# Reordering the first routing of a two-layer MoE kernel, with planner costs for a change of matmul shape

## The chip, the cores and the metric

The kernel runs on one core of one Trainium2 chip. The metric is the device time of one execution in microseconds. The kernel before takes 512.19 us (median of three runs, 511.12 to 512.78).

## The reference

The input `x` is 8 sequences of 256 rows of 128 numbers, 2,048 rows in all. Two layers follow; only the first is touched here. In shortened form:

```python
def moe(x):                                  # one weight set, used twice
    normed = rmsnorm(x) * norm_weight
    probs  = softmax(normed @ router.T)      # 8 experts
    w, idx = top_k(probs, 2); w /= w.sum()
    return x + alpha * sum_over_chosen(w_e * down_e(silu(gate_e(normed)) * up_e(normed)))

x = x + 0.5 * moe(layernorm(x))              # MoE layer r0
x = x + attention(layernorm(x))              # 16 heads of 8, causal
x = x + 0.5 * moe(layernorm(x))              # MoE layer r1
x = x + 0.5 * ffn(x); x = x + gated_shifts(x); x = x + 0.5 * ffn(x)   # the mixing stage
```

Each row goes to two of eight experts, so there are 4,096 pairs of a row and an expert, with a hidden size of 352.

## The kernel before, in words

**Groups and tiles.** The 2,048 rows are cut into four groups of 512 rows (`x[0]` to `x[3]`, each four tiles of 128 rows). An expert tile is 2 x 64 rows: the upper half belongs to one expert, the lower half to another. A MoE layer has 36 such tiles. The rows of each tile are gathered from memory by an index list (`take`), so the tiles can only begin when the list is known.

**Two plans in each MoE layer.** `moe_route(g, r)` normalises a group (`norm`), transposes it (`pt`), scales it (`nT`), computes the eight logits (`pl`) and takes the two topmost experts (`topmost`, the tiles `lg`, `top`, `which`). `moe_plan(r, False)` then builds the index list `take0` for the first 12 tiles from groups 0 and 1 alone; `moe_plan(r, True)` builds `take1` for the other 24 from all four groups. A plan is a chain of small steps on VectorE: marks (`wf`, `oh`, `m`), counts on TensorE (`pc`), a copy on ScalarE (`sums`), prefix sums on TensorE (`pp`), slots (`end` to `less`), `hit`, a product on GpSimd (`val`), comparisons `at` of 4 x 128 columns each (one set of the first plan on ScalarE, `ata`), and the sum `pi` on TensorE that turns them into `take`. Expert numbers come by a side path (`le`, `ef`, `pe`, `expert`).

**An expert tile.** `moe_experts` gathers (`xs`, an indirect DMA that GpSimd issues), transposes (`pt`), scales (`nT`). `moe_tile` copies the weights of the lower expert (`wg` 704 columns, `wd` 384 columns), multiplies (`pg`, `pu`, each as 64-row halves), applies Silu on ScalarE (`sg`), multiplies on VectorE (`hid`), transposes back on TensorE (`ph`), copies (`hT`) and multiplies down (`po`). `pg`, `pu` and `po` use 64 columns of the matmul array at a time; transposes and all other matmuls use another shape. A tile's `pg` is made to follow the `ph` of the tile two before it (line 1060).

**The order of the work.** Nothing waits in the program for what the planner writes: class `Work` (lines 117 to 253) is a list scheduler on the host. Each operation has an engine, an assumed cost and `needs`; its rank is the longest assumed path from it to the end, plus a bias (`w.back = -BIAS[..]`). `issue` picks the earliest start, or an operation of higher rank on the same engine that could start within 0.3 us of it. What comes out is the order of the instructions on each in-order engine. A need that is no real dependence therefore only moves an instruction in its queue. Where TensorE would stand idle, `keep_warm` issues dummy matmuls (`pw`). `either` lets the planner choose ScalarE or VectorE by the two costs given.

**Biases.** `BIAS[0..3]` lift the four groups in the last part of r1 and in the mixing stage, `BIAS[4]` the routing and first plan of r1, `BIAS[5]` its later groups and its whole plan, `BIAS[6]` the later groups and the whole plan of r0.

Of the kernel before, what the change touches and what calls it, by code (L numbers as in the profile page):

```python
# [19 lines left out]
P = 128  # L20
NG = 4
GT = 4
S = 256
E = 8
HID = 352
# [9 lines left out]

BIAS = (27.0, 38.0, 18.0, 10.0, 25.0, 29.0, 1.0)
HC = (0, 128, 224)
ROUND = float(3 * 2**22)  # L40
NH = 16
# [6 lines left out]
LN_EPS = 1e-5  # L48
RMS_EPS = 1e-6
# [58 lines left out]
class Op:  # L108
    def __init__(self, engine, us, do, needs, takes, uses, lag, spare):
        self.engine, self.us, self.do, self.lag, self.spare = engine, us, do, lag, spare  # L110
        self.takes, self.uses = takes, uses
        self.needs = [n for n in needs if n is not None]
        self.out, self.end, self.rank, self.back = None, None, None, 0.0
        self.choice = None


class Work:
# [9 lines left out]
    def __init__(self, buffers, free):  # L127
        self.ops, self.free, self.back = [], dict(free), 0.0
        self.buffers = {tag: [0.0] * n for tag, n in buffers.items()}
        self.idle = None  # L130

    def op(self, engine, us, do=None, needs=(), takes=(), uses=(), lag=0.0, spare=0):

# [22 lines left out]
    def start(self, op):  # L156
# [11 lines left out]
        op.engine, op.us = best[2], op.choice[best[2]]  # L168
        return best[1]

    def start_on(self, op):
        t = self.free.get(op.engine, 0.0)
        for n in op.needs:
            if isinstance(n, Op):
                t = max(t, n.end + self.gap(n, op))
        for buf in op.takes:
            slots = self.buffers[buf.tag]
            n = sum(b.tag == buf.tag for b in op.takes)
            if len(slots) < n + op.spare:
                return None  # L180
            t = max(t, sorted(slots)[n - 1])
        return t
# [5 lines left out]
    def keep_warm(self, a, b):  # L188
        slots = self.buffers["b"]
        us = self.WARM * (2 if a < self.COLD else 1)  # L190
        n = int((b - a - self.SLACK) / us)
        if n < 2 or min(slots) > a:
            return
        slots.remove(min(slots))
        slots.append(a + n * us)
        if self.idle is not None:
            self.idle(n)

    def issue(self):
        before = {}  # L200
        for op in self.ops:
            op.wait, op.rank = 0, 0.0
            before[op] = {n if isinstance(n, Op) else n.owner for n in op.needs} - {op}
            op.next = []
        for op in self.ops:
            op.wait = len(before[op])
            for n in before[op]:
                n.next.append(op)

        order, stack = [], [op for op in self.ops if op.wait == 0]  # L210
        left = {op: op.wait for op in self.ops}
        while stack:
            op = stack.pop()
            order.append(op)
            for n in op.next:
                left[n] -= 1
                if left[n] == 0:
                    stack.append(n)
        assert len(order) == len(self.ops), "operations need each other"
        for op in reversed(order):  # L220
            op.rank = op.us + max((n.rank + self.gap(op, n) for n in op.next), default=op.lag)
        for op in self.ops:
            op.rank -= op.back
        ready = [op for op in self.ops if op.wait == 0]
        while ready:
            starts = [(self.start(op), op) for op in ready]
            starts = [(t, op) for t, op in starts if t is not None]
            assert starts, "no buffer comes free"
            t, op = min(starts, key=lambda s: (s[0], -s[1].rank))
            for t2, op2 in starts:  # L230
                if op2.engine == op.engine and op2.rank > op.rank and t2 <= t + 0.3:
                    t, op = t2, op2
            ready.remove(op)
            if op.engine == "pe":
                self.keep_warm(self.free["pe"], t)
            for buf in op.takes:
                slots = self.buffers[buf.tag]
                slots.remove(min(slots))
            op.end = t + op.us
            if op.engine is not None:  # L240
                self.free[op.engine] = op.end
            if op.do is not None:
                op.out = op.do()
            for buf in (*op.uses, *(b for b in op.takes if b.left == 0)):
                buf.left -= 1
                buf.end = max(buf.end, op.end)
                if buf.left <= 0:
                    self.buffers[buf.tag].append(buf.end)
            for n in op.next:
                n.wait -= 1  # L250
                if n.wait == 0:
                    ready.append(n)
        return max(op.end for op in self.ops)
# [3 lines left out]
def tile_macaron(ctx: ExitStack, tc: tile.TileContext, a: dict, out: bass.AP):  # L257
# [22 lines left out]
    gu = ctile("gu", [P, E, 2 * HID])  # L280
    dw = ctile("dw", [P, E, len(HC), P])
# [18 lines left out]
    wd, wup, wuv, wo, wr, wkk, wv, vw, gw = (rest[:, c] for c in parts.values())  # L300
# [104 lines left out]
    def wtile(tag, name, shape, dtype=F32):  # L405
        return wk.tile(list(shape), dtype, tag=tag, name=name, bufs=len_of[tag])
# [17 lines left out]
    weights = w.op(None, 0.0, lag=24.0)  # L424
# [83 lines left out]
    def moe_layer(n, first):  # L508

        few = (4 * GT * first - 7) // 2  # L510

        soon = first + 1 if n == 1 and first + 1 < NG else None
        r = {
            "n": n, "first": first, "few": few, "soon": soon, "stored": {}, "all_stored": {}, "topped": {},
            "plan": {}, "hold": {},
        }
        for name, shape, dtype in (
            ("top", [P, NT, 8], F32), ("which", [P, NT, 8], U32), ("w", [P, NT, 2], F32),
            ("ab", [P, 2, NT], F32), ("rs", [P, NT], F32), ("slot", [P, 2 * NT], U32),
            ("take0", [P, few], U32), ("take1", [P, TILES - few], U32), ("expert", [1, 2 * TILES], I32),  # L520


            ("end", [P, E], F32), ("full", [P, 3, E], F32), ("base", [P, E], F32),
            ("both", [P, E], F32),
        ):
            r[name] = ctile(f"{name}_{n}", shape, dtype)
        for name, rows in (
            ("rows0", GT * first * P), ("rows1", NT * P), ("ys", TILES * P),
        ):
            r[name] = dram.tile([rows, P], F32, name=f"{name}_{n}", tag=f"{name}_{n}")  # L530
        return r

    def moe_route(g, r):


        n = 8 * r["n"] + g


        late = r["n"] == 0 and g >= 2
        y, filled = norm(  # L540
            g, n, "ep" if late else "y",
            (lambda: stile("ep", "ep", (P, 4, GT, P))[:, 0]) if late
            else lambda: wtile("y", "n", (P, GT, P)),
            eps=LN_EPS * RMS_EPS, scale=1.0 + RMS_EPS,
        )

        first = g < r["first"]
        to, rows = ("stored", "rows0") if first else ("all_stored", "rows1")
        aside = first and r["n"] == 0
        r[to][g] = (w.act if aside else w.sp)(  # L550
# [13 lines left out]
        b1, b2, nTb = Buf("b"), Buf("b"), Buf(tag)  # L564
# [26 lines left out]
                i = GT * g + t  # L591
                nc.vector.max_index(r["which"][:, i, :], r["top"][:, i, :], lg[:, t, :])

        r["topped"][g] = w.dve(1.3, topmost, pl, uses=[b2])

    def moe_weights(groups, r, behind):

# [58 lines left out]
    def moe_plan(r, whole):  # L656
# [248 lines left out]
        for k in range(2 * nt // GT):  # L905
            ab = Buf("ata" if k in by_act else "at")
            at = (w.act if k in by_act else w.dve)(
                1.6 if k in by_act else 0.68, lambda k=k: is_at(k), rowed, takes=[ab]
            )
            found = w.pe(  # L910
                0.3, lambda k=k, at=at: find(k, at), at, valued, found,
                **(dict(takes=[bi], uses=[ab]) if k == 0 else dict(uses=[ab, bi])),
            )
# [104 lines left out]
    def moe_tile(r, plan, k, nT, nb, j, pus, turned, downs, numbers):  # L1018
# [9 lines left out]
        def copied(engine, tag, src, width):  # L1028
            e = {"act": nc.scalar, "dve": nc.vector}[engine].number(
                r["expert"][0:1, 2 * k + 1 : 2 * k + 2]  # L1030
            )
            dst = wtile(tag, tag, (P, width))
            src = src[:, bass.ds(e, 1)].rearrange("p o h -> p (o h)")
            copies(engine, dst, src)
            return dst

        gb, db = Buf("wg"), Buf("wd")
        gates = w.either(
            1.15, 1.05, lambda e: copied(e, "wg", gu, 2 * HID), plan["experts"], weights,
            *pus[-3:-2], takes=[gb],  # L1040
        )
        backs = w.either(
            0.85, 0.76, lambda e: copied(e, "wd", dw.rearrange("p e c d -> p e (c d)"), len(HC) * P),
            plan["experts"], weights, *pus[-3:-2], takes=[db],
        )

# [14 lines left out]
                  takes=[bg], uses=[nb], spare=3)  # L1061
        pu = w.pe(0.6, lambda: product(1), pg, takes=[bu], uses=[nb, gb])
        pus.append(pu)

        def gate():
            sg = wtile("sg", "sg", (P, HID))
# [50 lines left out]

        po = w.pe(0.67, down, hT, backs, takes=[bo], uses=[tb, db])
        downs.append(po)

        def result(engine):
            ys = wtile("ys", "ys", (P, P))
# [755 lines left out]
```

## Time and profile before

| what | value |
|---|---|
| median of three runs | 512.19 us |
| the profiled execution | 510.68 us, of which span 508.5 us |
| TensorE busy | 485.4 us (95%), dummy matmuls included |
| VectorE, ScalarE, GpSimd busy | 351.0, 293.4, 224.9 us |
| first index list (`take`) written | at 24.91 us |
| first expert matmul (`pg`) | at 32.10 us |
| TensorE's work stops for r1's whole plan | 318.2 to 329.2 us, but for `pi` and `pe` |
| granted TensorE clock, mean | 0.98 |

The stages on this time axis: loading, routing and first plan of r0 up to 32 us; its expert tiles up to about 125 us; attention up to 300 us, with r1's first tiles among it from 285 us; r1's other tiles up to about 415 us; the mixing stage, overlapping, from about 406 us to the end. A row of the timeline reads: start in us, length in us, engine, line, operation, tile written<-tiles read, sizes, number of instructions merged into the row, and in brackets the idle time before it and what ended it.

### The profile page before, as it was taken

The page shows a single profiled execution, that of the slowest core. Times are in us where ns is not written, and L with a number is a line of the kernel's source. Part 1 is how long each engine was busy: PE and PEld are TensorE (multiplying, and loading weights), DVE is VectorE, ACT ScalarE, POOL GpSimd, SP SyncE. Part 2 cuts the span into 40 slices and gives each one's busy share as a digit, 9 for nine tenths or more (in the row PEclk, how much of TensorE's full clock was granted, in tenths as well). Part 3 has the DMA queues.
Part 4 walks back from the last instruction along what each step waited for, and adds up shares of the span by engine and source line. Part 5 has one row for each costly group of instructions (what it writes and reads, how often), then busy time and mean ns, then how long its engine had stood idle before and what let it go on. Part 6 is the DMA issues. An engine that isn't in the chain of part 4 may idle for free.

```text
span 508.5 us, 13883 instructions
## 1 busy us (share of the span) xinstructions
PE 485.4 (95%) x5206; PEld 312.9 (62%) x5206; DVE 351.0 (69%) x1217; ACT 293.4 (58%) x580; POOL 224.9 (44%) x240
## 2 busy tenths in 40 slices
PE   7978999999999999999999999599999998999995
PEld 4535666565666775776767766365666665566673
DVE  8788566476757986668786366935677755979770
ACT  3346676676355455455557566166767556586542
POOL 7084872563006600000027000278766568786731
PEclk9899999999999999999999999689999999999998
DMA  8941212231001100000201101022222111000001
GB/s 269 305 130 49 68 49 57 58 68 44 12 23 38 51 1 3 3 22 4 64 13 51 26 1 43 16 75 67 42 76 53 48 48 42 1 1 1 23 21 41
DMA packets 25984, 25.53 MB, mean 50 GB/s; under 512 B 3872, under 2 KB 23328, under 8 KB 25504
## 3 DMA queue, kind: packets, MB, share of 16 engines
q1 hardware_dynamic: 20368, 15.21, 9.7%
q0 software_dynamic: 4352, 8.92, 7.4%
q8 instruction: 42, 0.69, 0.6%
q10 hardware_dynamic: 1200, 0.53, 0.4%
q14 instruction: 22, 0.18, 0.1%
HBM read 16.78 MB, written 8.91 MB: 51 GB/s over the span
## 4 chain that ended last, share of the span: by engine, by line
PE 74%; DVE 11%; POOL 4%; issue 3%; ACT 1%; DMA 0%; POOLq 0%; ACTq 0%; DVEq 0%
PE sc L70 18%; PE po L70 15%; PE pg L70 9%; PE pu L70 9%; PE ph L70 6%; PE pt L70 5%; PE pgt L70 2%; DVE at L70 2%; PE pv L70 2%; POOL q L70 2%; PE pr L70 2%; PE pj L70 2%; POOL back L70 2%; DVE x L70 1%; PE pk L70 1%
## 5 line engine op out<-in xcount | busy, mean ns | idle before, releaser
L70 POOL DMA_INDIRECT xs<-rows,take x72 | 70.2, 976 | 48.3 <-issue 15.7
L70 POOL DMA_INDIRECT back<-ys,slot x64 | 61.3, 957 | 60.3 <-issue 45.4
L70 ACT ACTIVATE ep<-sc 128x512 f32<-128x512 f32 x96 | 52.3, 595 | 50.4 <-PE sc L70 46.8
L70 POOL TENSOR_TENSOR stats<-stats,minus_half 128x4 f32<-128x4 f32 x28 | 29.0, 1034 | 103.3 <-DVE stats L70 102.5
L70 DVE TENSOR_TENSOR hid<-sg,pu 128x352 f32<-128x352 f32 x71 | 36.8, 518 | 37.5 <-PE pu L70 35.9
L70 PEld LDWEIGHTS po<-dw,hT 128*64 128x64 f32 x432 | 49.9, 138 | 19.7 <-issue 15.9
L70 PE MATMUL po<-dw,hT 128*64 x432 | 60.0, 277 | 0.9 <-ACT sg L70 0.3
L70 PE MATMUL po<-wd,hT 128*64 128x128 f32 x432 | 60.1, 277 | 0.0
L70 ACT COPY wg<-gu 128x704 f32 x61 | 47.4, 779 | 19.7 <-PE pu L70 9.8
L70 PE MATMUL pg<-gu,nT 128*64 x144 | 57.4, 480 | 0.6 <-ACT nT L70 0.5
L70 PEld LDWEIGHTS sc<-kT,qT 32*128 32x128 f32 x768 | 46.0, 186 | 19.3 <-issue 17.3
L70 PE MATMUL pg<-wg,nT 128*64 128x352 f32 x144 | 57.4, 480 | 0.0
L70 PE MATMUL sc<-qT,kT 32*128 32x128 f32 x768 | 56.7, 283 | 0.0
L70 PE MATMUL pu<-wg,nT 128*64 128x352 f32 x144 | 56.2, 472 | 0.0
L70 PE MATMUL pu<-gu,nT 128*64 x144 | 56.2, 472 | 0.0
L70 PE MATMUL sc<-kT,qT 32*128 32x128 f32 x768 | 55.2, 284 | 0.0
L70 DVE TENSOR_REDUCE mtmp<-sc 128x4 f32<-128x512 f32 x64 | 41.4, 684 | 14.2 <-PE sc L70 14.0
L70 PEld LDWEIGHTS po<-wd,hT 128*64 128x64 f32 x432 | 49.9, 138 | 0.0
L70 PEld LDWEIGHTS sc<-qT,kT 32*128 32x128 f32 x768 | 47.4, 186 | 3.3 <-issue 2.1
L70 ACT ACTIVATE sg<-pg 128x352 f32<-128x352 f32 x72 | 33.4, 463 | 27.6 <-PE pg L70 22.3
L70 ACT COPY hT<-ph 128x384 f32<-128x384 f32 x56 | 26.7, 479 | 29.1 <-PE ph L70 27.5
L70 PE MATMUL ph<-ident,hid 128*128 128x128 f32 x216 | 39.2, 293 | 1.5 <-DVE hid L70 1.1
(227 smaller groups left out, 1056.1 us busy)
## 6 DMA issues: line engine op xcount, KB each, us to landing
ys<-ys SPq DMA_DIRECT2D x72, 64.0 KB, 1.5
gu<-in_guT SPq DMA_DIRECT2D x2, 1408.0 KB
rest<-in_rest SPq DMA_DIRECT2D x1, 1280.0 KB
xs<-rows,take POOLq DMA_INDIRECT x72
x<-in_x SPq DMA_DIRECT2D x4, 256.0 KB
dw<-in_dwT SPq DMA_DIRECT2D x1, 1024.0 KB
rows<-rows SPq DMA_DIRECT2D x2, 512.0 KB
back<-ys,slot POOLq DMA_INDIRECT x64
```

Of the source, the lines that this page charges most:

```text
L70: ins = do(*args, **kw)
```

## The change

Six edits, all in what the planner is told:

1. In `moe_route`, the moments of groups 2 and 3 of r0 are given a need on the normalised rows of groups 0 and 1 (`filled`).
2. The topmost experts of groups 2 and 3 of r0 are given a need on all comparisons `at`/`ata` of the first plan (`compared`).
3. `split=0` makes ScalarE normalise all four tiles of a group, where VectorE did two of them: groups 2 and 3 of r0, and groups 0 to 2 of r1.
4. The planner charges 0.1 us when TensorE changes between 64-column work (`strips`) and other work, and lets other work count as 0.1 us later still when it compares starts.
5. The assumed costs of the weight copies fall: `wg` from 1.15 and 1.05 us (ScalarE, VectorE) to 1.1 and 0.9, `wd` from 0.85 and 0.76 to 0.84 and 0.74.
6. The seven biases change.

```diff
-BIAS = (27.0, 38.0, 18.0, 10.0, 25.0, 29.0, 1.0)
+BIAS = (22.0, 28.0, 18.0, 12.0, 25.0, 34.0, -3.0)
...
+    SWITCH, STICK = 0.1, 0.1
+
     def start_on(self, op):
         t = self.free.get(op.engine, 0.0)
+        if op.engine == "pe" and op.us > 0.05 and op.strips != self.strips:
+            t += self.SWITCH
...
             starts = [(t, op) for t, op in starts if t is not None]
             assert starts, "no buffer comes free"
-            t, op = min(starts, key=lambda s: (s[0], -s[1].rank))
-            for t2, op2 in starts:
-                if op2.engine == op.engine and op2.rank > op.rank and t2 <= t + 0.3:
-                    t, op = t2, op2
+
+            starts = [
+                (t + self.STICK if op.engine == "pe" and op.strips != self.strips else t, t, op)
+                for t, op in starts
+            ]
+            at, t, op = min(starts, key=lambda s: (s[0], -s[2].rank))
+            for at2, t2, op2 in starts:
+                if op2.engine == op.engine and op2.rank > op.rank and at2 <= at + 0.3:
+                    at, t, op = at2, t2, op2
...
-            else lambda: wtile("y", "n", (P, GT, P)),
-            eps=LN_EPS * RMS_EPS, scale=1.0 + RMS_EPS,
+            else lambda: wtile("y", "n", (P, GT, P)), *r["filled"] if g >= r["first"] else (),
+            eps=LN_EPS * RMS_EPS, scale=1.0 + RMS_EPS, split=0 if late or r["n"] and g < NG - 1 else 2,
         )
 
         first = g < r["first"]
+        if first and r["n"] == 0:
+            r["filled"] += filled
...
-        r["topped"][g] = w.dve(1.3, topmost, pl, uses=[b2])
+        r["topped"][g] = w.dve(1.3, topmost, pl, *r["compared"], uses=[b2])
...
+            if r["n"] == 0 and not whole:
+                r["compared"].append(at)
...
         gates = w.either(
-            1.15, 1.05, lambda e: copied(e, "wg", gu, 2 * HID), plan["experts"], weights,
+            1.1, 0.9, lambda e: copied(e, "wg", gu, 2 * HID), plan["experts"], weights,
...
         backs = w.either(
-            0.85, 0.76, lambda e: copied(e, "wd", dw.rearrange("p e c d -> p e (c d)"), len(HC) * P),
+            0.84, 0.74, lambda e: copied(e, "wd", dw.rearrange("p e c d -> p e (c d)"), len(HC) * P),
...
         pus.append(pu)
+        pg.strips = pu.strips = True
...
         downs.append(po)
+        po.strips = True
```

The lines left out set `strips` to False at first, after dummy matmuls, and to that of the last TensorE operation issued.

More of the change, by code (lines that the diff above doesn't have):

```diff
@@ L113, in __init__ @@
         self.out, self.end, self.rank, self.back = None, None, None, 0.0
+        self.strips = False
         self.choice = None
@@ L129, in __init__ @@
         self.buffers = {tag: [0.0] * n for tag, n in buffers.items()}
-        self.idle = None
+        self.idle, self.strips = None, False
     def op(self, engine, us, do=None, needs=(), takes=(), uses=(), lag=0.0, spare=0):
@@ L195, in keep_warm @@
         slots.append(a + n * us)
+        self.strips = False
         if self.idle is not None:
@@ L235, in issue @@
                 self.keep_warm(self.free["pe"], t)
+                if op.us > 0.05:
+                    self.strips = op.strips
             for buf in op.takes:
@@ L514, in moe_layer @@
             "n": n, "first": first, "few": few, "soon": soon, "stored": {}, "all_stored": {}, "topped": {},
-            "plan": {}, "hold": {},
+            "plan": {}, "hold": {}, "filled": [], "compared": [],
         }
```

## Prediction

> **What bounds the kernel now.** I read the page's first two parts, then the chain that ended last, then the timeline of every stretch in which TensorE had no work of its own.
>
> ```profile
> PE 485.4 (95%) x5206; PEld 312.9 (62%) x5206; DVE 351.0 (69%) x1217; ACT 293.4 (58%) x580; POOL 224.9 (44%) x240
> PE   7978999999999999999999999599999998999995
> DVE  8788566476757986668786366935677755979770
> PEclk9899999999999999999999999689999999999998
> ```
>
> TensorE (PE) is the bound nearly everywhere: nines from 38 us on. The exceptions are the first three slices, one 5 at 318 to 330 us, and the end. But the first digits flatter it: until 32.1 us nearly all of its busy time is dummy matmuls (`pw`), so the first 32 us are a chain of small steps and no work of the experts. What that chain gains is carried to the end wherever TensorE has no slack: from 60 to 130 us it is busy 70.00 of 70 us, and from 130 to 190 us 59.78 of 60. So I ask first when the first expert matmul starts.
>
> ```profile
> 19.25 1.02 DVE L70 TENSOR_SCALAR at<-iota_r,row 128x128 f16<-128x128 f16 x4
> 20.20 0.18 DVE L70 COPY lg<-pl 128x32 f32<-128x32 f32 x1
> 21.24 0.17 DVE L70 COPY lg<-pl 128x32 f32<-128x32 f32 x1
> 22.28 1.37 DVE L70 TENSOR_SCALAR at<-iota_r,row 128x128 f16<-128x128 f16 x8
> 24.43 0.35 PE L70 MATMUL pi<-val,at 128*128 128x12 f16 x8
> 24.91 0.17 DVE L70 TENSOR_SCALAR take<-pi 128x12 uint32<-128x12 f32 x1 [0.93 <-PE pi L70]
> 25.39 1.32 POOL L70 DMA_INDIRECT xs<-rows,take  x1 [5.32 <-DVE wf L70]
> 31.34 0.30 PE L70 MATMUL pt<-ident,xs 128*128 128x128 f32 x1 [1.89 <-DMA xs<-rows,take]
> 32.10 0.51 PE L70 MATMUL pg<-gu,nT 128*64 x1 [0.46 <-ACT nT L70]
> ```
>
> Between the first comparison set and the other two, VectorE does the topmost experts of groups 2 and 3 (each begins with a `lg` copy): 20.20 to 22.28, 2.08 us that the first plan does not need. Then `pi` comes 0.78 us after the last `at` (23.65), since TensorE was inside 11 dummy matmuls until 24.4; they took 4.0 us, not the 2.2 us planned, because the granted clock was 0.50 between 22 and 24 us. `take` follows, the first gather, its landing, the first product.
>
> **Edit 2, topmost behind the comparisons.** With 2.08 us out of the way the two `at` sets run from 20.3 to about 21.7; ScalarE's set (`ata`) ends at 21.04 in this trace, so it is not late. The gap that called for the dummy matmuls shrinks from over 2 us to under 1, which gives back most of the 0.78: I take 0.6. `take` moves from 24.91 to 22.2, by 2.7 us (bounds 2.0 to 3.0). The moved instructions issue no DMA. Queued behind them on VectorE is the whole plan's first step (`wf`, at 25.00 now); 22.4 plus 2.08 is 24.5, so it is not later than before.
>
> **Edits 1 and 3 in r0.** Group 1's normalising on VectorE stood behind group 2's moments (7.01 to 8.27) though its own `pow` ended at 7.64. Moved, they give group 1 about 0.6 us, but its transposes then meet group 0's logits on TensorE (9.25 to 10.31), so 0.3 (0 to 0.6). The later `pow` steps stay hidden: GpSimd was idle from 11.8 to 19.4. On ScalarE, four tiles take 1.76 us in a block where two took 0.88. In this trace such a block (14.76 to 15.64) already held up the copy `sums` (15.55, its matmul having ended at 14.98) by about 0.3 us. Either that is cured or a block of 1.76 lands there: between +0.3 and -1.4; ScalarE was idle 3.24 us just before, and the first block fits in that gap, so I take 0. The rows' stores are issued by SP, which stood until 19.91 anyway. The Trainium skill (ScalarE: Activation LUTs, Rules for kernel authors) speaks against this edit: multiplies and adds belong on VectorE. By the rows VectorE needs 0.60 for two tiles and ScalarE 0.88. By the rule the later groups lose 0.3 us each; by the timeline nobody waits for them before the comparisons end, and VectorE gains 0.6 us each. I go by the timeline: 0. In r1 three groups move the same way inside attention, where ScalarE is busy 82.7 of 150 us and VectorE 102.3: 0 (plus or minus 0.5).
>
> **The gather's landing.** An earlier gather is worth something only if its rows land earlier.
>
> ```profile
> 329.42 1.05 POOL L70 DMA_INDIRECT xs<-rows,take  x1 [6.45 <-DVE take L70]
> ```
>
> That is the first gather of r1's second list, on an idle memory; the DMA view of 28 to 30 us (queue, packets, MB, share of the engines) is that of the first gather of all:
>
> ```profile
> q1 hardware_dynamic: 986, 0.50, 93.6%
> q0 software_dynamic: 12, 0.03, 3.6%
> ```
>
> At 329 us the first rows arrived 1.8 us after the issue and the gather was down within 2.6. At 25.39 it took 5.9 us: the gathers (q0) moved 12 packets before 30 us while SP's loads of `rest`, `gamma`, `beta` and two stores (q1) held 93.6% of the engines, and SP's traffic ended at 30.9. Read one way, the gather waits for that traffic to drain, and moving it earlier gains 0. The Trainium skill (DMA: Bandwidth & Descriptors, Queues, rings and completion order) says the other: each DMA engine takes turns between rings, packet by packet, so a gather needs no empty queue and the whole 3.0 us (2.7 and 0.3) arrives. The trace has it for SP and ScalarE: between 12.5 and 15 us ScalarE's stores moved packets one for one with SP's loads, though they too landed only after 7.2 us. I take 3.0, with 0 and 4 as ends.
>
> **From 32 to 45 us** TensorE does four tiles' products in 13 us, against one tile each 2.6 us later on (24 `pg` blocks from 48.5 to 108.7 us), because `hid` stands behind the whole plan on VectorE (a `hid` at 34.59 whose product ended at 33.5, one at 39.30 whose product ended at 37.6). The -4 in `BIAS[6]` lets `hid` pass. What it delays is the second list (`take` at 46.56), needed for the 13th tile near 66 us: over 10 us of cover. 0.5 us (0 to 2).
>
> **Edit 4, changes of shape.** A start-to-start step across a change of shape against one without:
>
> ```profile
> 310.08 0.27 PE L70 MATMUL po<-dw,hT 128*64 x1
> 310.30 0.55 PE L70 MATMUL ph<-ident,hid 128*128 128x128 f32 x3
> ...
> 313.62 0.27 PE L70 MATMUL po<-dw,hT 128*64 x1
> 313.73 0.46 PE L70 MATMUL pg<-gu,nT 128*64 x1
> ```
>
> 0.22 against 0.11: a change costs 0.1 us (0.15 going into 64-column work, whose first step is also 0.34, not 0.29). I count 178 changes in the whole trace. But each of 72 tiles has a `ph` of its own between `pu` and `po`, which needs two; and rank still decides when both kinds are ready. I expect some 10 fewer: 1.0 us (-1 to 3).
>
> **Edits 5 and 6.** `wg` on VectorE takes 528 ns (11 of 72), on ScalarE 779; at the new costs more go to VectorE. In 60 to 130 us both are near 65% busy and TensorE never waits: 0 (plus or minus 1). `BIAS[0..3]` keep their order (group 1, 0, 2, 3) with less spread; the mixing stage loses 1.0 us on TensorE in 380 to 400, 1.5 in 420 to 440 and some 6 in the last 8.5 us: 0 (plus or minus 2.5), I see no side. `BIAS[5]` is a rival below.
>
> **Sum.** 3.0 + 0.5 + 1.0 = 4.5 us; I drop 0.3 for what the start does not pass on. The profiled execution would go from 510.68 to 506.5 (span 508.5 to 504.3, with the 2.2 us around it); the median of the runs, 1.5 us above the profiled one, from 512.2 to 508.0.
>
> **Rivals.**
> *The landing is hidden* (chance 0.17). The first gather still lands at 31 us behind SP's traffic; only 1.0 us from the changes of shape remains: 511.2.
> *More at both stops* (0.15). `hid` passing the plan fills another 2 us of 32 to 45, and 20 fewer changes another 2: 504.0.
> *The second layer's stop grows* (0.18, slower).
>
> ```profile
> 317.92 0.27 PE L70 MATMUL po<-dw,hT 128*64 x1
> 322.24 0.26 PE L70 MATMUL pi<-val,at 128*128 128x24 f16 x3 [4.04 <-DVE at L70]
> 329.19 0.87 PE L70 MATMUL ph<-ident,hid 128*128 128x128 f32 x3 [0.42 <-DVE take L70]
> 330.16 0.48 ACT L70 COPY hT<-ph 128x384 f32<-128x384 f32 x1 [10.36 <-PE ph L70]
> ```
>
> From 313.4 to 328.4 VectorE runs r1's whole plan without a break; two finished products wait for `hid`, TensorE stops for 11 us, with three of the 12 tiles unstarted, and the granted clock is 0.5 from 321 to 334.7. Five more in `BIAS[5]` can put the plan ahead of yet more `hid`. Each tile pushed behind the stop costs 2.6 us afterwards, unless the plan also ends earlier. From two tiles on it eats the gain; three give 512.2 - 4.2 + 7.8 = 515.8. Against it: the plan already outranked these tiles, since none passed it.
> *The forecast* (0.50), alone 505.5 to 510.5.
>
> **How the numbers follow.** About 0.3% (1.5 us) is what a measurement can tell from no change. The forecast is faster in 0.48 of its 0.50, the next best all 0.15, the hidden landing 0.03 faster, 0.11 same, 0.03 slower; the grown stop 0.01 same, 0.17 slower; 0.02 of the forecast is same. Faster 0.66, same 0.14, slower 0.20. The range 503.5 to 514.5 takes in the hidden landing, most of the better case and the grown stop with two tiles.
>
> **What would show it.** Right: `take` near 22.2, the first `pg` near 29, no `lg` between the `at` sets, fewer than 170 changes of shape, the stop of r1 3 to 5 us earlier and no longer. Wrong: a first gather landing at 31 us again; `sums` behind a 1.76 us block; fewer `pg` before r1's stop. I would be most wrong if the later queues, all reordered by the new costs, lost more than the start gives.

## The result and the profile after

The changed kernel takes 509.72 us (median of 6 runs, 507.72 to 511.09) against 511.95 us before on the same chip: ratio 0.9955, 95% interval 0.9937 to 0.9972. It is faster by 2.2 us, half of the 4.2 forecast. Ratios leave out slow executions (over 1.5% above the fastest of the same kernel), so they can differ a little from the ratio of two medians. The profiled execution happens to be the slowest of the six (511.09 us, span 509.4), so its times must not be set against the median. A second profile of the changed kernel, unaltered (507.65 us, span 505.9, called "changed, again" below), is of the fastest of 22 executions. Read together, the two show what belongs to the kernel and what to one execution.

The page of the changed kernel, its busy times and slices of the span:

```profile
PE 491.5 (96%) x5196; PEld 316.1 (62%) x5196; DVE 348.1 (68%) x1202; ACT 295.5 (58%) x595; POOL 224.6 (44%) x240
PE   7989999999999999999999999899999997999995
PEclk9779999999999999999999999789999999899998
```

The 5 of the second layer's stop has become an 8, but with 16 dummy matmuls; a 7 has appeared in the slice at 420 to 433 us; and the granted clock has a 7 in the second and third slice, where it had 8 and 9. Rows of the timeline of TensorE and VectorE over the start show what that did:

```profile
10.11 2.79 PE L70 MATMUL pl<-few,nT 128*128 128x8 f32 x16
12.75 4.85 PE L70 MATMUL pw<-before,ones_b 128*128 128x512 bf16 x11
14.64 0.22 DVE L70 TENSOR_TENSOR m<-oh 128x64 bf16<-128x64 f32 x1
17.53 0.32 PE L70 MATMUL pc<-ones_b,m 128*64 128x128 bf16 x1
28.36 4.63 PE L70 MATMUL pw<-before,ones_b 128*128 128x512 bf16 x13
32.83 0.22 PE L70 MATMUL pc<-ones_b,m 128*128 128x128 bf16 x1
```

`pc`, the first step of the first plan, had its input `m` at 14.86 but stood behind dummy matmuls until 17.53: eleven of them, from 12.75 on, took 0.4 us each at half clock where 0.22 had been planned. The same happened again in front of the whole plan's `pc` at 32.83; `take` came at 25.30, the first `pg` at 34.04. So this execution lost on the clock what the reordering had won. Rows of "changed, again":

```profile
18.61 2.33 DVE L70 TENSOR_SCALAR at<-iota_r,row 128x128 f16<-128x128 f16 x12
21.20 0.18 DVE L70 COPY lg<-pl 128x32 f32<-128x32 f32 x1
22.24 0.15 DVE L70 TENSOR_SCALAR take<-pi 128x12 uint32<-128x12 f32 x1
22.70 1.27 POOL L70 DMA_INDIRECT xs<-rows,take  x1 [3.27 <-DVE until L70]
25.21 4.26 PE L70 MATMUL pw<-before,ones_b 128*128 128x512 bf16 x13
29.30 0.22 PE L70 MATMUL pc<-ones_b,m 128*128 128x128 bf16 x1
31.38 0.30 PE L70 MATMUL pt<-ident,xs 128*128 128x128 f32 x1 [1.86 <-DMA xs<-rows,take]
32.14 0.51 PE L70 MATMUL pg<-gu,nT 128*64 x1 [0.32 <-DMA rows<-ep]
```

Here the plan is early: all twelve `at` in one piece with no `lg` between them, `take` at 22.24 against 24.91 before. One group's topmost experts (the `lg` at 21.20 begins them) now stand between the comparisons, done at 20.94, and `take`. And still the first product starts at 32.14, where it was 32.10 before. The 2.7 us are gone between the gather's issue and its landing. In the DMA view (queue, packets, MB, share of the engines) from 25.5 to 28 us the gathers move half a tile's 64 KB, and SP's loads and stores hold 86% of the engines:

```profile
q1 hardware_dynamic: 79, 0.68, 86.2%
q0 software_dynamic: 9, 0.03, 2.8%
```

**Where the 2.2 us come from.** I cut both traces at three matmuls: the first product `pg`, the last score `sc` of attention, and the first `pg` after the second layer's stop. Up to the third cut, the stretches hold the same work apart from dummies; only with the charge alone is one tile less begun before it. Times in us:

| kernel (one execution each) | first `pg` | to the last `sc` | to the first `pg` after r1's stop | to the end | span |
|---|---|---|---|---|---|
| before | 32.10 | 258.57 | 39.33 | 178.49 | 508.49 |
| after | 34.04 | 257.72 | 37.83 | 179.79 | 509.38 |
| changed, again | 32.14 | 257.99 | 37.83 | 177.98 | 505.94 |
| first layer only | 33.68 | 259.55 | 39.34 | 178.12 | 510.69 |
| charge for shape only | 33.20 | 258.69 | 37.38 | 186.42 | 515.69 |
| biases only | 32.54 | 260.63 | 39.34 | 182.98 | 515.49 |

The start gives nothing. The second layer's stop gives 1.50 us, alike in both executions of the changed kernel and the largest part of the 2.55 us by which "changed, again" is shorter than the kernel before. Rows of the kernel before at the end of the stop:

```profile
328.55 0.50 DVE L70 TENSOR_TENSOR hid<-sg,pu 128x352 f32<-128x352 f32 x1
330.00 0.85 PE L70 MATMUL pg<-gu,nT 128*64 x1
```

And after:

```profile
319.38 3.63 PE L70 MATMUL pw<-before,ones_b 128*128 128x512 bf16 x16
322.84 0.23 PE L70 MATMUL pi<-val,at 128*128 128x24 f16 x3
324.98 0.52 DVE L70 TENSOR_TENSOR hid<-sg,pu 128x352 f32<-128x352 f32 x1
325.65 0.87 PE L70 MATMUL ph<-ident,hid 128*128 128x128 f32 x3 [0.18 <-DVE hid L70]
326.32 3.35 PE L70 MATMUL pi<-val,at 128*128 128x24 f16 x24
329.59 0.85 PE L70 MATMUL pg<-gu,nT 128*64 x1
```

Before, that `hid` stood on VectorE behind all comparisons of the plan, `ph` had to wait for it until 329.19 (the row in the prediction names `take`, which came after `hid`), and `pg` came 0.81 us behind. Now one tile's `hid` passes the plan's last 24 comparisons, its `ph` lies inside the wait, and `pg` follows `pi` directly. The rest may be dummies: from the first `pg` to the last `sc` the planner puts in 15, not 19, and after the stop 12, not 20 (of which 20 and 6 stand in the last 25 us). At 0.22 us, 12 fewer are 2.6 us at most, an estimate; how many of them stood in the way of work is not shown.

Against that stands a new wait in the mixing stage, where before the longest was 1.49 us. TensorE's timeline of "changed, again":

```profile
425.65 1.46 PE L70 MATMUL pw<-before,ones_b 128*128 128x512 bf16 x6
429.74 1.47 PE L70 MATMUL pt<-ident,y 128*128 128x128 f32 x4 [2.63 <-DVE p L70]
```

Six dummies and 2.63 us of idle time, and right behind it the clock is at half for 3.4 us (430.6 to 434.0).

### The profile page after: what moved, and what is told of

Read it like the earlier page. It is cut to its first block, busy times and chain, and to the rows that moved or that the text cites. A ratio compares the mean times of both kernels' runs of the same rounds, so it can differ in the third digit from the quotient of the medians.

```text
span 509.4 us, 13872 instructions
## 1 busy us (share of the span) xinstructions
PE 491.5 (96%) x5196; PEld 316.1 (62%) x5196; DVE 348.1 (68%) x1202; ACT 295.5 (58%) x595; POOL 224.6 (44%) x240
## 4 chain that ended last, share of the span: by engine, by line
PE 81%; DVE 5%; POOL 2%; issue 2%; DMA 2%; ACT 1%; POOLq 0%; ACTq 0%; DVEq 0%
PE sc L70 18%; PE po L70 16%; PE pg L70 9%; PE pu L70 8%; PE ph L70 6%; PE pt L70 5%; PE pgt L70 5%; PE pv L70 3%; PE pr L70 3%; PE pk L70 2%; PE pj L70 2%; POOL back L70 2%; DMA xs<-rows,take 1%; PE pi L70 1%; DVE at L70 1%
## 5 line engine op out<-in xcount | busy, mean ns | idle before, releaser
L70 ACT COPY wg<-gu 128x704 f32 x58 | 45.2, 779 | 17.0 <-PE pu L70 12.2
L70 ACT ACTIVATE sg<-pg 128x352 f32<-128x352 f32 x72 | 33.4, 464 | 27.9 <-PE pg L70 23.0
L70 PEld LDWEIGHTS ph<-ident,hid 128*128 128x128 f32 x216 | 23.2, 143 | 26.7 <-issue 11.6
```

The source lines that it names most:

```text
L70: ins = do(*args, **kw)
```

## The experiments

The first four ran on one chip, where the kernel before takes 511.36 us. The other eight ran on chips where the kernel before itself takes 591 to 599 us, with pauses of engines that no releaser in the profile explains; only ratios on one chip are compared there, and the profiles are used for the first 33 us and for the stop, which look alike on all chips. The changed kernel itself was not timed on those chips, so what runs 5 to 12 gain or lose against it is known only through their ratios to the kernel before.

**1. The changed kernel again,** unaltered.

> The changed kernel once more, unaltered, for a second profile. Theory (phase): its first product at 34.0 us came from two stretches of half clock (11.3 to 18.1 and 24.9 to 31.8 us) that lie elsewhere in another execution; then the first product comes 1 to 4 us earlier than 34.0 and the time is near 509.7. Rival (fixed): the start is really later than before, the first product is again near 34 us and the gain is made somewhere behind it.

510.2 us, ratio 0.9976 (0.9963 to 0.9989; 22 runs from 507.65 to 511.79). The gain is real and small: 1.2 to 2.2 us by the two measurements. The first product came 1.9 us earlier than in the first profile, as the theory had it. The spread of 4.1 us goes with the clock: the five executions with the lowest mean granted clock (0.970) took 511.3 to 511.8 us, the two with the highest (0.980) 507.7 and 508.8. Half clock was granted at 11.3 to 18.1 and 24.9 to 31.8 us in the one profile, at 21.0 to 27.9 in the other. The changed kernel also gets less of the clock: 18 of its 22 executions were granted 0.976 or less, and 2 of 35 of the kernel before. At 0.979 to 0.980 four of the one took 507.7 to 509.7 us and fourteen of the other 510.5 to 513.0, so the order by itself may be worth more than the medians show.

**2. First layer only.** The kernel before with the waits of edits 1 and 2 and ScalarE's normalising in r0:

```
+ *r["filled"] if g >= r["first"] else (), split=0 if late else 2
+ r["topped"][g] = w.dve(1.3, topmost, pl, *r["compared"], uses=[b2])
```

> The kernel before with the first layer's edits alone (moments and topmost of groups 2 and 3 behind the first plan, their rows by ScalarE; no change-of-shape cost, old costs and biases). Theory: the start is what gained, ratio 0.993 to 0.997. Rival (changes of shape) and rival (biases): 0.998 to 1.002.

512.28 us, ratio 1.0009 (0.9994 to 1.0024). No gain. In its profile `take` comes at 27.20, later than before. A half clock (12.0 to 15.4 us) has a part in it, but the order has too: 18 dummies stand before `pc`, and both groups' topmost experts now stand between the comparisons and `take`. VectorE's rows:

```profile
22.87 2.33 DVE L70 TENSOR_SCALAR at<-iota_r,row 128x128 f16<-128x128 f16 x12
25.12 0.18 DVE L70 COPY lg<-pl 128x32 f32<-128x32 f32 x1
26.16 0.17 DVE L70 COPY lg<-pl 128x32 f32<-128x32 f32 x1
27.20 0.15 DVE L70 TENSOR_SCALAR take<-pi 128x12 uint32<-128x12 f32 x1
```

Run 7 below has the same order; there half clock begins only at 21.3, and `take` comes at 25.52, still later than the 24.91 before.

**3. The charge for a change of shape only,** and **4. the biases only,** each in the kernel before:

```
+ SWITCH, STICK = 0.1, 0.1    (and strips = True on pg, pu and po)
```
```
-BIAS = (27.0, 38.0, 18.0, 10.0, 25.0, 29.0, 1.0)
+BIAS = (22.0, 28.0, 18.0, 12.0, 25.0, 34.0, -3.0)
```

> The kernel before with the planner's charge for a change of matmul shape alone. Theory (start gained): ratio 0.998 to 1.002, since the changed kernel has as many changes of shape (178) as the one before. Rival (changes of shape): 0.994 to 0.997.

> The kernel before with the seven new biases alone. Theory (start gained): ratio 0.997 to 1.003. Rival (biases made the gain, in the mixing stage): 0.994 to 0.997. Rival of the prediction (the second layer's stop grows by BIAS[5]): 1.003 or more.

515.56 us, ratio 1.0073 (1.0046 to 1.0100), and 517.73 us, ratio 1.0115 (1.0093 to 1.0137). Each alone makes the kernel slower, though the two are in a kernel that is faster. For run 3 neither range had allowed that; for run 4 the last rival had, but not by the way it named. The table shows where: both lose after the stop, 7.93 and 4.49 us. With the charge alone only 8 tiles have their `pg` before the stop, not 9; after it there are twelve more `po` and the `pg`, `pu` and `ph` of the tile left over, 29 dummies for 20, ten more changes of shape (188 in the whole trace, not 178), and TensorE waits 4.7 us, not 3.2. With the biases alone the stop is unchanged (39.34), and the mixing stage has three waits for VectorE's `p`. TensorE's timeline of that kernel, 430 to 446 us:

```profile
435.39 1.32 PE L70 MATMUL pt<-ident,y 128*128 128x128 f32 x4 [1.67 <-DVE p L70]
442.15 1.13 PE L70 MATMUL pgt<-yTg,rest 128*128 128x512 f32 x2 [1.93 <-DVE p L70]
444.44 1.59 PE L70 MATMUL pgt<-yTg,rest 128*128 128x512 f32 x2 [1.15 <-DVE p L70]
```

4.75 us of waiting here, where the kernel before has 1.49 and the changed one 2.63. Its 2.1 us in the stretch up to the last `sc` lie beside a half clock from 31.9 to 38.8; where TensorE has work throughout, 6.9 us at half clock cost 3.4, an estimate.

**5. to 7. The changed kernel with one part undone:** its first-layer edits (edits 1 to 3, here the changed pieces of three lines), its charge for shape, its biases.

```
-*r["filled"] if g >= r["first"] else (),
+*(),
-split=0 if late or r["n"] and g < NG - 1 else 2,
+split=2,
-r["topped"][g] = w.dve(1.3, topmost, pl, *r["compared"], uses=[b2])
+r["topped"][g] = w.dve(1.3, topmost, pl, uses=[b2])
```
```
-SWITCH, STICK = 0.1, 0.1
+SWITCH, STICK = 0.0, 0.0
```
```
-BIAS = (22.0, 28.0, 18.0, 12.0, 25.0, 34.0, -3.0)
+BIAS = (27.0, 38.0, 18.0, 10.0, 25.0, 29.0, 1.0)
```

> The changed kernel with the first layer's edits undone (needs on filled and compared taken out, split 2 everywhere). In the last profiles the gather was issued 2.7 us earlier than before and yet landed at the same 31.4 us. Theory (landing hidden, gain made in the expert tiles): 0.995 to 1.000, as the changed kernel, with the first gather issued near 25 and landed near 31.4. Rival (the start gained): 1.000 to 1.005.

> The changed kernel with the charge for a change of matmul shape set to 0. Theory (the charge makes the gain of 2 us between the first product and attention, alone it did so too): the first scores come at 124.5 to 127 us instead of 123, and the ratio is 1.000 to 1.006. Rival (the biases or the start): 0.995 to 0.999.

> The changed kernel with the old seven biases. Theory (the biases only fit the end of the second layer to the new order): the first scores near 123 us as in the changed kernel, and all of a loss behind 330 us, ratio 1.001 to 1.010. Rival (biases do nothing): 0.995 to 0.999.

Ratios to the kernel before on the same chip: 0.9986 (0.9961 to 1.0011), 1.0160 (1.0103 to 1.0217) and 1.0073 (1.0043 to 1.0103). Without the first layer's edits no loss can be told from the noise. Nor does the early list need them. VectorE's rows in run 5:

```profile
19.43 2.32 DVE L70 TENSOR_SCALAR at<-iota_r,row 128x128 f16<-128x128 f16 x12
22.00 0.18 DVE L70 COPY lg<-pl 128x32 f32<-128x32 f32 x1
23.05 0.15 DVE L70 TENSOR_SCALAR take<-pi 128x12 uint32<-128x12 f32 x1
```

From the first comparison to `take` it is 3.62 us here, 3.62 with the biases alone (run 4), 3.63 in the changed kernel, 4.33 with the first layer's edits and old biases (runs 2 and 7), 5.66 before, and 4.78 in the order of before where no half clock fell into it (run 3). The biases alone put the topmost experts of groups 2 and 3 behind the comparisons. Without either of the other two, the kernel is slower than before, by about as much as the one that remains cost alone in runs 3 and 4 (1.0073 for 1.0073, 1.0160 for 1.0115). So the gain needs both; edit 5 was in all three kernels, and the pair without it was not tried. The stretch with the stop takes 39.78 us without the charge and 37.83 with the charge and the old biases (run 7), and with the charge alone a `hid` passes the comparisons too: it comes from the charge. In run 7 nine tiles get ahead of the stop, not the eight of run 3, and it is slower by as much: the tile left over can't be all that the charge costs alone.

**12. The changed kernel without its charge, on another chip,** the edit of run 6.

> The changed kernel without the charge for a change of shape, once more, for the same reason. Theory (the charge and the biases make the gain together, in the expert tiles of both layers): first scores at 124.5 us or later, ratio 1.003 to 1.016. Rival (that ratio of 1.016 belonged to the slow chip): 0.996 to 1.001.

1.0115 (1.0038 to 1.0192), with the same 39.79 us at the stop; the loss did not belong to the one chip.

**8. A late `rest`.** The gather shares its time with SP's transfers. In the changed kernel, `rest`, and `gamma` and `beta` behind it, are loaded after the first gathers:

```
-rest_loaded = w.sp(1.5, load_rest, *(r0["stored"][g] for g in first), lag=8.0)
+rest_loaded = w.sp(1.5, load_rest, r0["plan"][1]["taken"], lag=8.0)
```

> The changed kernel with SP's loads of rest, gamma and beta issued only when the second list of the first layer is written. Theory (the landing of the first gather is held by these loads): the gather lands within 3 to 4 us of its issue, the first product comes 3 us earlier, near 29 us or before in an execution with an early first list, and the ratio is 0.990 to 0.994. Rival (the gather is slow for another reason, or the stretch behind it is bound otherwise): the landing stays near 31 us or the first scores do not move, 0.996 to 1.000.

1.0032 (1.0007 to 1.0057). This is slower than before, where a gain was expected. The gather, issued at 22.61, has moved 0.06 MB by 26 us, about a tile's 64 KB. The DMA view from 25 to 26:

```profile
q0 software_dynamic: 28, 0.06, 23.9%
```

Yet TensorE, in the timeline:

```profile
25.48 5.71 PE L70 MATMUL pw<-before,ones_b 128*128 128x512 bf16 x13
30.98 0.30 PE L70 MATMUL pc<-ones_b,m 128*128 128x128 bf16 x1
31.09 0.31 PE L70 MATMUL pt<-ident,xs 128*128 128x128 f32 x1
```

`pt` no longer waits for the DMA. It stands in TensorE's queue behind `pc`, and that behind 13 dummies, which the planner had put at 2.8 us and which took 5.5. A second cover lay under the first.

**9. Half the dummies:** the changed kernel with `COLD` 34.0 for 9.0, by which the planner counts on a colder TensorE and fills less (6 for 13 here, the order of the rest unchanged).

> The changed kernel with half as many dummy matmuls up to 34 us (14, 5, 3, 0, 6 and 3 where it has 14, 11, 7, 3, 13 and 7); all else in the same order. Theory (two covers in a row, the landing behind SP's loads at 31 us and 13 dummy matmuls at half clock until 29 to 31 us): the first list no longer slips to 25 us when the clock is halved, but the first product stays at 32 us since the landing holds it, ratio 0.995 to 0.998 with less spread than the changed kernel. Rival (the dummies alone held the start): first product near 29 us, 0.989 to 0.993. Rival (fewer dummies cost more clock): slower than the changed kernel, 0.999 or more.

1.0059 (1.0021 to 1.0097). `pc` comes at 28.03, but now `pt` waits for the landing again, until 31.80, and `pg` starts at 32.71. Taken away alone, neither cover gains anything at the start. The ratio fits the rival that fewer dummies cost clock: half clock lasts from 14.0 to 37.9 us in this profile, in run 8 from 20.9 to 31.1.

**10. and 11. Both together,** on two chips.

> The changed kernel with half the dummy matmuls up to 34 us and with SP's loads of rest, gamma and beta only when the first layer's second list is written. Theory (two covers in a row): with both gone the first rows land near 26 us, the first product comes at 28.5 to 29.5 us, and 2 to 3 us of it reach the end, ratio 0.988 to 0.993. Rival (what is gained at the start is lost again on the way, in the plan's share of VectorE or at a later landing): first product early but first scores at 122.5 us or later, 0.995 to 0.999.

> The same kernel as the last (SP's loads of rest, gamma and beta late, half the dummy matmuls up to 34 us), once more, since the last two calls ran on chips where the kernel before took 591 and 599 us. There its first product came at 29.4 us instead of 32.7, but stops of several us without a visible cause hid what became of it. Theory (the start passes on): where the kernel before takes 511 us, first product at 29 to 29.5, first scores near 120 us, ratio 0.990 to 0.994. Rival (given back on the way): first scores at 122.5 or later, 0.995 to 0.999.

TensorE's timeline in run 10:

```profile
28.05 0.31 PE L70 MATMUL pc<-ones_b,m 128*128 128x128 bf16 x1
28.15 0.42 PE L70 MATMUL pt<-ident,xs 128*128 128x128 f32 x1
29.36 0.82 PE L70 MATMUL pg<-gu,nT 128*64 x1 [0.22 <-issue]
```

With both gone the first product starts at 29.36 (29.87 in run 11), which is where the forecast had put it. But the time is 1.0047 (1.0016 to 1.0079) and 0.9986 (0.9948 to 1.0023): on these chips the 3 us are not seen in the time. In run 10 they are gone by the first score of attention, 155.91 us against 155.81 in run 9. A pause like this one stands between, on ScalarE and on TensorE behind it:

```profile
37.50 0.37 ACT L70 ACTIVATE nT<-pt,few 128x128 f32<-128x128 f32 x1 [5.07 <-remote]
37.92 0.85 PE L70 MATMUL pg<-gu,nT 128*64 x1 [5.43 <-issue]
```

In both runs half clock was granted beyond the first product too (to 30.4 and again from 37.2 to 44.0 us in run 10), so the missing dummies are a second suspect. Whether the 3 us would arrive on a chip without such pauses was not tried.

## Why the prediction was half right

- **What bounds the kernel:** held. TensorE is the bound from the first product on, and the first 32 us are a chain of small steps.
- **Edit 2, topmost behind the comparisons:** the number was right to a tenth of a microsecond, by luck. `take` was to come at 22.2 and came at 22.24 where the clock had been full until 21.0. But the edit by itself does not bring it (27.20 and 25.52 in runs 2 and 7), and without it the list comes at 23.05 (run 5), by the biases. Two errors also met: the comparisons began 0.64 us earlier than before (18.61 for 19.25), and a group's topmost experts, 1.04 us, slipped in behind them and before `take`.
- **The gather's landing, "I take 3.0, with 0 and 4 as ends":** this is the step that failed. 0 was right. The rule that I leaned on (the Trainium skill, DMA: Bandwidth & Descriptors, Queues, rings and completion order: each engine takes turns between rings packet by packet) says that a gather need not wait for an empty queue; it does not say that it is quick. Issued at 22.70 with SP's transfers about, it was 8.7 us until `pt`; with `rest`, `gamma` and `beta` moved away a tile's rows were through within about 3.5. The row of 25.39 us, 12 packets in two microseconds, had shown this, and I let the rule outvote it. The rival "the landing is hidden" had the mechanism, for one half: I had not seen that TensorE's own queue, with the whole plan's `pc` and its dummies ahead of `pt`, hides the landing a second time (runs 8 to 10).
- **Edit 1 at 0.3, edit 3 at 0:** nothing against it in the time; together with edit 2 they are 1.0009 put in and 0.9986 with them taken out. At the start the comparisons begin at 18.5 to 18.6 us with them and at 19.3 to 19.6 without, in profiles whose clock is full up to there; with the old biases they begin later (21.20 in run 7). There the sign of being wrong came, `sums` behind a block of four tiles on ScalarE (it starts at 16.48, as the block ends). Edit 3 in r1 was not tried by itself. VectorE is busy 111.8 of 150 us there (130 to 280 us), not 102.3; nothing hung on it.
- **`hid` passing the plan, 0.5 us:** the mechanism was there, at both ends. In the 13 us from the first product TensorE is idle 0.6 us in both profiles after, 1.6 before. Little of it lasts: up to the last `sc` it is 2.31 and 2.55 us after, 2.27 before, and that stretch is shorter by 0.6 to 0.9 us, which four dummies fewer could explain. At the second layer's stop, where I had put no gain, the `hid` that passes saves 1.50 us; there the charge does it, not `BIAS[6]`.
- **`BIAS[6]`, cover of the second list:** held. `take` of the second list came at 53.1 to 54.8, not 46.56, and no product waited for it.
- **Changes of shape, 10 fewer for 1.0 us:** wrong. There are 178 before and 178 after. The charge alone makes 188; the changed kernel without it has 184. It works as another order of the queue more than through the number of changes.
- **The rival "second layer's stop grows":** did not come about in the changed kernel (9 tiles before the stop, as before). Its mechanism is real, though: with the charge alone it is 8 tiles, and run 3 is 0.73% slower. I had hung it on `BIAS[5]`; with the biases alone the stop stays as it was.
- **Edits 5 and 6 in the mixing stage, "0 (plus or minus 2.5), I see no side":** the biases alone lose 4.5 us after the stop and the charge alone 7.9; together they lose 1.3 in one profile and gain 0.5 in the other. That parts do not add was missing from the sum: 1.0009, 1.0073 and 1.0115 would make +2%, and the whole is -0.2 to -0.45%.

So the side was right by luck: most of the 4.2 us forecast (3.0 of a sum of 4.5) was to come from a start that gave nothing, and by the table the 1.2 to 2.2 us measured come from the order behind it, above all from the `hid` that passes at the second stop. That order I had at 1.5 us, with one mechanism right but in another place and one wrong. What stays open: why the charge and the biases mend each other's loss. The traces show what each loses (a tile behind the stop; waits for `p` in mixing) and that both are smaller when they meet, not which decision of the planner does it. Edit 5 is in all kernels with two parts and in none with one, so that it has a share can't be excluded; with one part beside it (runs 6 and 7) it did not help. After the stop, up to 1.5 us of a difference in the table (run 4) is not accounted for by tiles, dummies, waits, changes of shape and clock.

## What to carry to other kernels

Before a step is paid for coming earlier, list everything that its consumer stands behind, in the memory and in its own engine's queue; each cover has to go, and taking away one shows nothing. Before an edit is given the credit for an order, see whether another edit makes the same order without it. An edit to the costs of an order that a planner works out is a draw from many orders: measure the parts together and apart, since two that lose alone can win together, and count what fills the gaps (dummy matmuls) as work on the path, at the slow clock's price. When a forecast is about 3 us and one execution of the kernel differs from another by 4, read two profiles before believing either.

## What the hardware showed that I had not expected

- The clock of TensorE: inside the span, half clock came in stretches of 3.4 us and their multiples (3.4, 6.8, 10.2, 13.7), at a different place in two executions of one kernel, and also while TensorE was busy (11.3 to 18.1 us, busy 6.55 of 6.8 us with `pl` of 8 columns and dummies). The Trainium skill (TensorE: Matmul & The Clock Gate, Part 1) has the free-running window of 3.4 us. What it does to a queue was new to me: dummies that are there to keep the clock up are at their longest (0.4 us for 0.22) exactly when they have failed, and then they hold up the plan by 2 to 3 us.
- One chip runs the kernel before in 511 us, others in 591 to 599, at a granted clock of 0.92 to 0.94 for 0.98, with pauses of 5 us of which the profile names no cause. A ratio carries over only roughly: one kernel (runs 6 and 12) has 1.0160 on one of the slower chips and 1.0115 on another, another (runs 10 and 11) 1.0047 and 0.9986, each pair with intervals that overlap.
